# A graph network in four layers: norms, scores, logits and attention rows made group by group

## The chip, the cores and the metric

The kernel runs on one core of a Trainium2 chip. A core has TensorE (PE in the profile; its weight loads are listed apart as PEld), VectorE (DVE), ScalarE (ACT), GpSimd (POOL) and SyncE (SP, which here only issues transfers). Each takes its instructions from a queue of its own, in order, and waits there for semaphores. The metric is the device time of one execution in microseconds, the median of several.

## The reference

The input is a table of 3125 nodes with 256 features, 100,000 edges, and a second list of 65,536 edges. Eight layers follow one another; each normalises the rows (no weights), computes something, and adds it to x:

```
x += gat2(norm(x))          two attention layers with one head, over the edges and self loops
x += moe0(norm(x))          scores = n @ Wg + bg; two of 8 experts, gelu
x += norm(x) @ W            W is a 256x256 matrix set from the edge weights
x += moe1(norm(x))          routing by a 4-head attention over the second list; two of 4 experts
x += channel(norm(x))       s = n @ Wself + b; softmax per channel over a node's edges
x += moe2(norm(x))          rh = relu(n @ w1 + b1); scores = softmax(rh @ w2 + b2); two of 6
x += gat8(norm(x))          attention with 8 heads of 32, relu
x += moe3(norm(x))          the tokens are added too; scores = n @ rw; two of 8, gelu
```

An attention sums, for each node, the rows of its sources with weights exp(leaky_relu(a_src + a_dst)), divided by the sum of the weights. The channel layer does the same for each of the 256 channels apart, with weights that depend only on the source. An expert layer takes for every node the two experts with the highest scores and adds their two outputs, in most layers with a gate.

## The kernel before, in words

Nodes are padded to 3200: 25 tiles of 128 rows, in five groups of five (`GT`, `NG`), or for the multi-head attentions in seven chunks of up to four (`CHUNKS`). x stays on chip as 25 tiles of 128x256. The normalised table is kept transposed in `xT`.

`norm_group(g, then)` normalises one group: five `bn_stats` and five `bn_aggr` on DVE (L181, L183), the reciprocal square root over DVE, ACT and DVE (L184 to L186), the shift (L187), and then for each of the five tiles the normalised tile `xn` on ACT (L190), two transposes on PE (L166), their copy to `xT` on ACT (L167), and `then(t, xn)`. `xn` has five buffers, the transposes' banks `tr` two; `acc` has six. `layer_norm` (L195) runs the five groups one after another.

Edges are held as a dense table of counts in device memory, 3200x3200. `aggregate` (one head) and `channels` go over five groups of target tiles; for each they run over all 25 source tiles, load a strip of counts (L261, four buffers, on SP's queue), and collect into five accumulator banks by matmul (L294 in the first, L1406 in the second); then each of the five tiles is finished on DVE. In `aggregate_heads` (multi-head) a chunk of four tiles takes four passes over the sources with two heads each; of ten units seven form their weights on DVE (L366) and three on ACT and POOL (L360, L361, L363), and the matmul is L368. Strips of counts (L324) stay for the four passes in 25 + `kept` buffers; `kept` is 8 in the last attention. At the fourth source of the next chunk the chunk's sums are transposed back (L339) and finished (L1477 to L1482).

`gat_prepare` makes what an attention needs: weights with attention columns (L205 to L211), then for every tile the projected row (four PE matmuls at L221, a copy on ACT at L223, one on DVE at L224), and then the maximum, the exponentials and the scaling (L228 to L251).

`experts` sorts the nodes by expert, gathers rows with indirect transfers on POOL, runs the experts on PE, scatters results, and at its end combines: for each tile a load of two result rows (L680) and two DVE instructions that add them to x (L685). After each group it calls `after(g)`. `keep_row` (L444) writes a normalised tile to the table that is gathered from; it issues on SP.

A planner orders the instructions of PE, DVE, ACT and SP by modelled times. It takes the earliest in program order among those it believes ready, so it can pull later work into idle time of an engine; POOL keeps the order of the program. The channel aggregation stands in a branch on the edge data (`tc.If`), and nothing moves across the branch.

The seams in question, with their lines: after the second attention `layer_norm(keep_row)` (L1269) and `project` for 25 tiles (L432, L437); after the second expert layer's combine the logits of the channel layer (L1377, L1380, L1382, L1383; the exponentials are L1387 and the transposes back L1391); after the channel aggregation `layer_norm` and a two-layer router (L1452, L1455, L1458, L1459); after the third expert layer's combine `gat_prepare`; after the last attention `layer_norm(add_tokens)`, whose extra DVE addition is L1491, and `project` (L432, L435).

Of the kernel before, what the change touches and what calls it, by code (L numbers as in the profile page):

```python
# [41 lines left out]
AF = mybir.ActivationFunctionType  # L42
ALU = mybir.AluOpType
# [34 lines left out]
def gnn_moe_kernel(ctx: ExitStack, tc: tile.TileContext, a, out):  # L78
# [120 lines left out]
    def gat_prepare(pool, inT, w, att_src, att_dst, heads, hd, width, loops):  # L199
# [18 lines left out]
        for t in range(T):  # L218
            ps = acc_bank()
            for k in range(KD):  # L220
                nc.tensor.matmul(ps[:, :f + 2 * heads], inT[:, k, t * P:(t + 1) * P], waug[:, k, :],  # L221
                                 start=(k == 0), stop=(k == KD - 1))
            nc.scalar.copy(mov[:, t, :, 0:hd], ps[:, :f].rearrange("p (h d) -> p h d", h=heads))  # L223
            nc.vector.tensor_copy(elr[:, t, :], ps[:, f:f + 2 * heads])  # L224
        el, er = elr[:, :, 0:heads], elr[:, :, heads:]
# [31 lines left out]

    def load_counts(pool, s, c0, n):

        ct = new(pool, [P, GT * P], "ct", bufs=4)[:, :n * P]  # L260
        nc.sync.dma_start(ct, view(cnt_1)[s * P:(s + 1) * P, c0 * P:(c0 + n) * P])  # L261
        return ct
# [19 lines left out]
    def aggregate(pool, mov, q, r, finish, background):  # L282


        for g in range(NG):
# [10 lines left out]
            for j in range(GT):  # L296
                finish(g * GT + j, acc[j])

# [128 lines left out]
    def project(dst, w_sb, e, bias=None):  # L427

        for t in range(T):
            ps = tr_bank()  # L430
            for k in range(KD):
                nc.tensor.matmul(ps[:, :e], xT[:, k, t * P:(t + 1) * P], w_sb[:, k, :],  # L432
                                 start=(k == 0), stop=(k == KD - 1))
            if bias is None:
                nc.vector.tensor_copy(dst[:, t, :], ps[:, :e])  # L435
            else:
                nc.vector.tensor_add(dst[:, t, :], ps[:, :e], bias)  # L437
# [740 lines left out]
    quick.close()  # L1178
    with tc.tile_pool(name="gat1", bufs=1) as gp:
# [6 lines left out]
        aggregate(gp, mov, q, r, finish, background)  # L1186
# [80 lines left out]
    rows, keep_row = token_rows(0)  # L1267
    rows1, keep_row1 = token_rows(1)
    layer_norm(keep_row)  # L1269
    with tc.tile_pool(name="moe0", bufs=1) as mp:  # L1270
        e = 8
        wg = new(mp, [P, KD, e], "wg")
        nc.sync.dma_start(wg, a["L0_ffn_Wg"].rearrange("(k p) e -> p k e", p=P))
        bg = bcast(a["L0_ffn_bg"], e, mp, "bg")
        score = new(mp, [P, T, e], "score")
        project(score, wg, e, bg)
        oh1, _, oh2, _ = top_two(mp, score, e)

        def after0(g):
            norm_group(g)  # L1280
            for t in range(g * GT, (g + 1) * GT):
# [8 lines left out]
                a["L0_ffn_W2"], a["L0_ffn_b2"], AF.Gelu, after0, meanwhile)  # L1290
    some_left = nc.values_load(flag[0:1, 2:3], min_val=0, max_val=1)
# [5 lines left out]
    with tc.tile_pool(name="route1", bufs=1) as rp:  # L1297
# [4 lines left out]
        with tc.tile_pool(name="gat_r", bufs=1) as gp:  # L1302
# [46 lines left out]
            for kept, v in zip(hot + gate, (oh1, oh2, m1, m2)):  # L1349
                nc.vector.tensor_copy(kept, v)  # L1350
        with tc.tile_pool(name="moe1", bufs=1) as mp:
            experts(mp, rows1, list(zip(hot, gate)), e, [(a["L1_ffn_W1"], a["L1_ffn_b1"], 512)],
                    a["L1_ffn_W2"], a["L1_ffn_b2"], AF.Gelu, norm_group)


    with tc.tile_pool(name="chan", bufs=1) as cp:
# [7 lines left out]
        with tc.tile_pool(name="self", bufs=1) as sp:  # L1364
            ws = new(sp, [P, KD, D], "ws")
            nc.sync.dma_start(ws, a["L2_gnn_W_self"].rearrange("(c p) k -> p c k", p=P))
            wsT = new(sp, [P, KD, D], "wsT")
            for c in range(KD):
                transpose_to(wsT, c, ws[:, c, :])
            bs = columns(sp, a["L2_gnn_b_self"].rearrange("(c p) -> c p", p=P), KD, "bs")  # L1370
            eT = new(sp, [P, KD, NP], "eT")
            top = new(sp, [P, KD], "top")
            for c in range(KD):
                for t0, n in CHUNKS:
                    ps = acc_bank()
                    for k in range(KD):
                        nc.tensor.matmul(ps[:, :n * P], wsT[:, k, c * P:(c + 1) * P],  # L1377
                                         xT[:, k, t0 * P:(t0 + n) * P],
                                         start=(k == 0), stop=(k == KD - 1))
                    nc.scalar.activation(eT[:, c, t0 * P:(t0 + n) * P], ps[:, :n * P], AF.Identity,  # L1380
                                         bias=bs[:, c:c + 1])
                nc.vector.tensor_reduce(top[:, c:c + 1], eT[:, c, :], AX.X, ALU.max)  # L1382
# [5 lines left out]
            for t in range(T):  # L1388
# [6 lines left out]
                split(sp, mov[0][:, t], mov[1][:, t], both)  # L1395

        def channels(pool, parts_of):

            for g in range(NG):
# [9 lines left out]
                for j in range(GT):  # L1409
# [12 lines left out]
                    nc.vector.tensor_add(x[:, t, :], x[:, t, :], o)  # L1422

# [14 lines left out]
    rows, keep_row = token_rows(2)  # L1438
    layer_norm(keep_row)
    with tc.tile_pool(name="moe2", bufs=1) as mp:  # L1440
        e = 6
        rw1 = new(mp, [P, KD, P], "rw1")
        nc.sync.dma_start(rw1, a["L2_ffn_router_w1"].rearrange("(k p) h -> p k h", p=P))
        rw2 = new(mp, [P, e], "rw2")
        nc.sync.dma_start(rw2, a["L2_ffn_router_w2"])
        rb1 = columns(mp, a["L2_ffn_router_b1"].rearrange("(c p) -> c p", p=P), 1, "rb1")
        rb2 = bcast(a["L2_ffn_router_b2"], e, mp, "rb2")
        score = new(mp, [P, T, e], "score")
        for t0, n in CHUNKS:
            ps = acc_bank()  # L1450
            for k in range(KD):
                nc.tensor.matmul(ps[:, :n * P], rw1[:, k, :], xT[:, k, t0 * P:(t0 + n) * P],  # L1452
                                 start=(k == 0), stop=(k == KD - 1))
            rh = new(mp, [P, 4 * P], "rh", bufs=2)
            nc.scalar.activation(rh[:, :n * P], ps[:, :n * P], AF.Relu, bias=rb1)  # L1455
            for j in range(n):
                pl = tr_bank()
                nc.tensor.matmul(pl[:, :e], rh[:, j * P:(j + 1) * P], rw2, start=True, stop=True)  # L1458
                nc.vector.tensor_add(score[:, t0 + j, :], pl[:, :e], rb2)  # L1459
# [5 lines left out]
                a["L2_ffn_expert_w3"], a["L2_ffn_expert_b3"], AF.Relu, norm_group)  # L1465


    with tc.tile_pool(name="gat3", bufs=1) as gp:
        h, hd = 8, 32
        _, q, r, _, flat = gat_prepare(gp, xT, a["L3_gnn_W"].rearrange("f h d -> f (h d)"),  # L1470
                                   a["L3_gnn_att_src"], a["L3_gnn_att_dst"], h, hd, 64, False)
        bias = bcast(a["L3_gnn_bias"], D, gp, "bias")

        def finish(t, sums):
# [7 lines left out]
            nc.vector.scalar_tensor_tensor(x[:, t, :], o, 0.0, x[:, t, :], op0=ALU.max, op1=ALU.add)  # L1482

        aggregate_heads(gp, lambda s: view(cnt_1)[s * P:(s + 1) * P], flat, q, r, h, hd + 1, 64, finish, (2, 5, 8), 8)


    rows, keep_row = token_rows(3)

    def add_tokens(t, xn):
        keep_row(t, xn)  # L1490
        nc.vector.tensor_add(x[:, t, :], x[:, t, :], xn)  # L1491
# [6 lines left out]
    layer_norm(add_tokens)  # L1498
    with tc.tile_pool(name="moe3", bufs=1) as mp:
        e = 8  # L1500
        rw = new(mp, [e, D], "rw")
        nc.sync.dma_start(rw, a["L3_ffn_router_w"])
        ps = tr_bank()
        for k in range(KD):
            nc.tensor.transpose(ps[:, k * e:(k + 1) * e], rw[:, k * P:(k + 1) * P], ident[:e, :e])
# [67 lines left out]
```

## Time and profile before

| what | value |
|---|---|
| median of 3 runs | 4291.32 us (4287.93 to 4295.2) |
| the profiled execution, its own time | 4283.67 us |
| its span | 4281.9 us |
| PE, DVE, POOL, ACT busy | 81%, 59%, 45%, 34% |
| mean granted TensorE clock | 0.866 |

The span is from the first to the last instruction of the one execution that was profiled. A line of the timeline gives the start and length in us, engine, source line, operation, output<-inputs and count; in brackets the idle time of the engine before it and what ended that. A line of the waits gives who waited for whom, the us in all, how often, and the longest.

### The profile page before, as it was taken

What the parts mean: (1) busy time and instruction counts of PE and PEld (TensorE: products, weight loads), DVE (VectorE), ACT (ScalarE), POOL (GpSimd) and SP (SyncE); (2) the same over time, 40 slices, a digit from 0 to 9 for tenths busy, and PEclk for the clock granted to TensorE, in tenths of its full rate; (3) what the DMA queues carried; (4) which work ended last, traced back from release to release, by engine and by line L of the source; (5) the groups of instructions that cost most, each with busy time, mean ns of one, the idle gap of its engine ahead of it and who ended that gap; (6) DMA issues with size and microseconds to landing.
All of it is one profiled execution on the core that took longest, in us unless ns stands there. A gap on an engine that the chain in (4) does not pass through costs nothing. (4 is left out here: it accounts for less than half of the span.)

```text
span 4281.9 us, 49111 instructions
## 1 busy us (share of the span) xinstructions
PE 3461.9 (81%) x15922; PEld 2276.5 (53%) x15922; DVE 2529.1 (59%) x6325; ACT 1472.6 (34%) x2767; POOL 1929.4 (45%) x1581
## 2 busy tenths in 40 slices
PE   0348988799969976999699588959959999996883
PEld 0247777678837755333477267726733333344452
DVE  7789887655443123999411623262249999997223
ACT  0212212110011224898122500022238888884010
POOL 4226667777704420777243000004507777771352
PEclk9967787799959996999799699968979999996796
DMA  7455554456615654341364244415641211101345
GB/s 262 189 161 112 127 126 87 65 107 150 130 52 158 184 145 140 118 129 48 91 182 142 63 127 121 137 55 150 184 162 59 65 62 62 47 11 46 88 152 151
DMA packets 369627, 497.83 MB, mean 116 GB/s; under 512 B 85279, under 2 KB 253288, under 8 KB 369348
## 3 DMA queue, kind: packets, MB, share of 16 engines
q1 hardware_dynamic: 240304, 345.54, 27.0%
q0 software_dynamic: 83808, 88.11, 10.0%
q10 hardware_dynamic: 45236, 60.81, 4.1%
q8 instruction: 132, 2.16, 0.2%
q14 instruction: 147, 1.20, 0.1%
HBM read 402.61 MB, written 132.68 MB: 125 GB/s over the span
## 5 line engine op out<-in xcount | busy, mean ns | idle before, releaser
L363 POOL TENSOR_TENSOR p_pool<-most,ct 128x512 f32<-128x512 f32 (+1 forms) x630 | 730.9, 1163 | 487.1 <-ACT most L361 291.8
L366 DVE SCALAR_TENSOR_TENSOR p<-acc,r,ct 128x512 f32<-128x512 f32 (+1 forms) x1470 | 909.0, 686 | 40.4 <-PE acc L368 22.4
L368 PE MATMUL acc<-p,mov 128*64 128x512 f32 (+3 forms) x2940 | 910.6, 561 | 24.3 <-DVE p L366 24.3
L629 POOL DMA_INDIRECT xg<-rows,slot x244 | 245.5, 1006 | 889.0 <-PE tr L604 546.1
L368 PE MATMUL acc<-p_pool,mov 128*64 128x512 f32 (+3 forms) x1260 | 595.0, 558 | 4.3 <-POOL p_pool L363 3.7
L368 PEld LDWEIGHTS acc<-p,mov 128*64 128x64 f32 (+1 forms) x2940 | 289.5, 128 | 398.3 <-DVE p L366 236.4
L656 ACT ACTIVATE hT<-acc,bias 128x256 f32<-128x256 f32 x424 | 199.4, 473 | 818.8 <-PE acc L654 818.8
L360 ACT ACTIVATE most<-qb,minus_r 128x512 f32<-128x512 f32 (+1 forms) x630 | 423.3, 672 | 118.4 <-POOL p_pool L363 109.9
L669 POOL DMA_INDIRECT results<-ys,home x244 | 238.1, 976 | 458.3 <-DMA results<-ys,home 218.6
L361 ACT ACTIVATE most<-most,r 128x512 f32<-128x512 f32 (+1 forms) x630 | 424.6, 676 | 16.8
L811 POOL DMA_INDIRECT cnt_2a<-val,idx x192 | 319.8, 1666 | 238.8 <-DVE last L776 108.6
L811 POOL DMA_INDIRECT cnt_2b<-val,idx x192 | 324.6, 1691 | 128.7 <-DMA cnt_2b<-val,idx 71.3
L654 PE MATMUL acc<-gT_in,w 128*128 128x256 f32 x1456 | 362.1, 398 | 25.2 <-DVE gT_in L648 25.2
L664 PE MATMUL acc<-wl,hT 128*128 128x256 f32 x1456 | 381.6, 395 | 0.0
L659 DVE CAST own_hot<-mine 64x128 fp32r<-64x128 f32 x122 | 27.0, 222 | 513.0 <-PE acc L662 512.8
L654 PEld LDWEIGHTS acc<-gT_in,w 128*128 128x128 f32 x1456 | 282.5, 199 | 76.1 <-DVE gT_in L648 36.3
L1174 PE MATMUL acc<-mov,p 128*128 128x257 f32 x1250 | 304.7, 406 | 2.9 <-DVE p L279 2.9
L664 PEld LDWEIGHTS acc<-wl,hT 128*128 128x128 f32 x1456 | 257.7, 190 | 53.8 <-issue 0.7
L294 PE MATMUL acc<-mov,p 128*128 128x257 f32 x1250 | 273.1, 381 | 6.1 <-DVE p L279 6.1
L1174 PEld LDWEIGHTS acc<-mov,p 128*128 128x128 f32 x1250 | 250.4, 204 | 50.5 <-DVE p L279 10.2
L1406 PE MATMUL acc<-mov_high,ct 128*128 128x512 f32 x625 | 250.9, 401 | 30.6 <-DVE o L1418 15.3
L294 PEld LDWEIGHTS acc<-mov,p 128*128 128x128 f32 x1250 | 237.9, 191 | 40.9 <-DVE p L279 6.8
(394 smaller groups left out, 4763.9 us busy)
## 6 DMA issues: line engine op xcount, KB each, us to landing
ct<-cnt SPq DMA_DIRECT2D x250, 320.0 KB
rows<-cnt ACTq DMA_DIRECT2D x12, 3200.0 KB
cnt<-rows ACTq DMA_DIRECT2D x12, 3200.0 KB
ct<-cnt SPq DMA_DIRECT2D x150, 256.0 KB
w<-in_L_ffn_W SPq DMA_DIRECT2D x60, 512.0 KB
wl<-in_L_ffn_W SPq DMA_DIRECT2D x60, 512.0 KB
yg<-results SPq DMA_DIRECT2D x100, 256.0 KB
rows<-ktab SPq DMA_DIRECT2D x48, 512.0 KB
```

What stands on the lines that cost most here:

```text
L294: nc.tensor.matmul(acc[j][:, :D + 1], p[:, j * P:(j + 1) * P], mov[:, s, 0, :], start=(s == 0), stop=(s == T - 1))
L360: nc.scalar.activation(most, copy[:, h, :n * P], AF.Relu, bias=minus_r[:, s, head:head + 1])
L361: nc.scalar.activation(most, most, AF.Identity, bias=r[:, s, head:head + 1])
L363: nc.gpsimd.tensor_mul(p, most, ct)
L366: nc.vector.scalar_tensor_tensor(p, banks[h][:, :n * P], r[:, s, head:head + 1], ct, op0=ALU.max, op1=ALU.mult)
L368: nc.tensor.matmul(acc[h * width:(h + 1) * width, :n * P], mov[:, s, head * wide:head * wide + width], p, start=(s == 0), stop=(s == T - 1))
L629: nc.gpsimd.indirect_dma_start(out=gathered[i][:, h, :], out_offset=None, in_=rows[:, :], in_offset=bass.IndirectOffsetOnAxis(ap=slot[:, i ...
L654: nc.tensor.matmul(ph[:, :ROWS], ws[n][:, k, c * P:(c + 1) * P], src[:, k, :], start=(k == 0), stop=(k == k_in - 1))
L664: nc.tensor.matmul(py[:, h * D:(h + 1) * D], src[:, k, h * P:(h + 1) * P], ws[-1][:, k, :], start=False, stop=(k == k_in - 1))
L811: nc.gpsimd.indirect_dma_start(out=table[:, :], out_offset=bass.IndirectOffsetOnAxis(ap=idx[:, t:t + 1], axis=0), in_=val[:, t:t + 1], in_ ...
L1174: nc.tensor.matmul(acc[j][:, :D + 1], p[:, j * P:(j + 1) * P], mov[:, s, 0, :], start=(s == 0), stop=(s == T - 1))
L1406: nc.tensor.matmul(acc[j], part[:, j * P:(j + 1) * P], mov[k][:, s, :], start=(s == 0 and i == 0 and k == 0), stop=(s == T - 1 and i == le ...
```

## The change

`gat_prepare` is cut into `gat_begin`, which loads weights and returns a function that makes one tile's row, and `gat_end`. `project` does one tile. `aggregate` takes a function that it calls after each group. With these, five pieces of work are called from the stage ahead, group by group: norm and scores of the first expert layer from the second attention; the logits of the channel layer from the second expert layer's combine; norm and router of the third expert layer from inside the branch of the channel aggregation; the last attention's rows from the third expert layer's combine; norm, token addition and scores of the last expert layer from the `finish` of the last attention. The pools that hold what they make are opened earlier, and `kept` in the last attention goes from 8 to 7. The logits' maximum is taken per group and channel half, and then over the groups.

```diff
-        for t in range(T):
+
+        def tile_of_rows(t):
             ps = acc_bank()
...
+        return tile_of_rows, (heads, hd, mov, elr, flat)
...
-    def aggregate(pool, mov, q, r, finish, background):
+    def aggregate(pool, mov, q, r, finish, after, background):
...
                 finish(g * GT + j, acc[j])
+            after(g)
...
+    def scored0(t, xn):
+        keep_row(t, xn)
+        project(score0, wg, 8, t, bg)
...
-        aggregate(gp, mov, q, r, finish, background)
+        aggregate(gp, mov, q, r, finish, lambda g: norm_group(g, scored0), background)
...
-    layer_norm(keep_row)
...
-        project(score, wg, e, bg)
-        oh1, _, oh2, _ = top_two(mp, score, e)
+        oh1, _, oh2, _ = top_two(mp, score0, e)
...
+        def logits(g):
+            norm_group(g)
+            for c in range(KD):
+                for t0, n in ((g * GT, 3), (g * GT + 3, 2)):
+                    ps = acc_bank()
+                    for k in range(KD):
+                        nc.tensor.matmul(ps[:, :n * P], wsT[:, k, c * P:(c + 1) * P], xT[:, k, t0 * P:(t0 + n) * P],
+                                         start=(k == 0), stop=(k == KD - 1))
+                    nc.scalar.activation(eT[:, c, t0 * P:(t0 + n) * P], ps[:, :n * P], AF.Identity, bias=bs[:, c:c + 1])
+                nc.vector.tensor_reduce(tops[:, c, g:g + 1], eT[:, c, g * GW:(g + 1) * GW], AX.X, ALU.max)
...
-                    a["L1_ffn_W2"], a["L1_ffn_b2"], AF.Gelu, norm_group)
+                    a["L1_ffn_W2"], a["L1_ffn_b2"], AF.Gelu, logits)
...
+    def scored2(g):
+        norm_group(g, keep_row2)
+        for t0, n in ((g * GT, 3), (g * GT + 3, 2)):
+            ps = tr_bank()
+            for k in range(KD):
+                nc.tensor.matmul(ps[:, :n * P], rw1[:, k, :], xT[:, k, t0 * P:(t0 + n) * P],
+                                 start=(k == 0), stop=(k == KD - 1))
+            rh = new(rp2, [P, 3 * P], "rh", bufs=2)
+            nc.scalar.activation(rh[:, :n * P], ps[:, :n * P], AF.Relu, bias=rb1)
+            for j in range(n):
+                pl = tr_bank()
+                nc.tensor.matmul(pl[:, :6], rh[:, j * P:(j + 1) * P], rw2, start=True, stop=True)
+                nc.vector.tensor_add(score2[:, t0 + j, :], pl[:, :6], rb2)
...
                     nc.vector.tensor_add(x[:, t, :], x[:, t, :], o)
+                scored2(g)
...
-    layer_norm(keep_row)
...
+    rows_gat3, begun3 = gat_begin(last_gat.enter_context(tc.tile_pool(name="gat3_rows", bufs=1, side="right")),
+                                  xT, a["L3_gnn_W"].rearrange("f h d -> f (h d)"),
+                                  a["L3_gnn_att_src"], a["L3_gnn_att_dst"], h3, hd3, 64)
...
-                a["L2_ffn_expert_w3"], a["L2_ffn_expert_b3"], AF.Relu, norm_group)
+                a["L2_ffn_expert_w3"], a["L2_ffn_expert_b3"], AF.Relu,
+                lambda g: norm_group(g, lambda t, xn: rows_gat3(t)))
...
+    def scored3(t, xn):
+        keep_row3(t, xn)
+        nc.vector.tensor_add(x[:, t, :], x[:, t, :], xn)
+        project(score3, rwT, 8, t)
...
-        _, q, r, _, flat = gat_prepare(gp, xT, a["L3_gnn_W"].rearrange("f h d -> f (h d)"),
-                                   a["L3_gnn_att_src"], a["L3_gnn_att_dst"], h, hd, 64, False)
+        _, q, r, _, flat = gat_end(gp, begun3, False)
...
             nc.vector.scalar_tensor_tensor(x[:, t, :], o, 0.0, x[:, t, :], op0=ALU.max, op1=ALU.add)
+            if t % GT == GT - 1:
+                norm_group(t // GT, scored3)
 
-        aggregate_heads(gp, lambda s: view(cnt_1)[s * P:(s + 1) * P], flat, q, r, h, hd + 1, 64, finish, (2, 5, 8), 8)
+        aggregate_heads(gp, lambda s: view(cnt_1)[s * P:(s + 1) * P], flat, q, r, h, hd + 1, 64, finish, (2, 5, 8), 7)
...
-    layer_norm(add_tokens)
...
-        project(score, rwT, e)
```

## The prediction

> **What bounds the kernel now.** I read the page first: no engine bounds the whole.
>
> ```profile
> PE 3461.9 (81%) x15922; PEld 2276.5 (53%) x15922; DVE 2529.1 (59%) x6325; ACT 1472.6 (34%) x2767; POOL 1929.4 (45%) x1581
> PEclk9967787799959996999799699968979999996796
> ```
>
> The stages follow each other and each has its own bound, so the second view is the table of busy time by stretch, over each stage and the seam behind it. Columns: stretch, its length, busy us of PE, PE's weight load, DVE, ACT, POOL (instructions), granted clock, DMA share, GB/s.
>
> ```profile
> 892.00:1173.00 281.00, 276.26 (x1273) 240.39 (x1274) 142.75 (x262) 11.17 (x26) 210.96 (x124) 0.99 0.69 146
> 1173.00:1211.00 38.00, 33.18 (x145) 26.93 (x144) 12.38 (x59) 14.50 (x38) 8.56 (x6) 0.57 0.24 57
> 2359.00:2391.00 32.00, 12.90 (x40) 5.79 (x40) 30.74 (x108) 17.17 (x43) 0.00 (x0) 0.50 0.64 192
> 2391.00:2426.00 35.00, 27.41 (x72) 12.93 (x71) 10.27 (x18) 14.90 (x29) 0.00 (x0) 0.84 0.00 0
> 2472.00:2790.00 318.00, 297.80 (x1250) 238.94 (x1250) 81.10 (x165) 0.00 (x0) 0.00 (x0) 0.96 0.45 128
> 2790.00:2846.00 56.00, 30.42 (x129) 20.35 (x130) 33.72 (x128) 26.25 (x64) 0.00 (x0) 0.71 0.18 62
> 3133.00:3166.00 33.00, 12.98 (x40) 5.79 (x40) 30.74 (x107) 17.45 (x44) 0.00 (x0) 0.50 0.62 186
> 3166.00:3204.00 38.00, 28.62 (x110) 21.83 (x110) 9.67 (x44) 14.38 (x38) 0.00 (x0) 0.79 0.71 246
> 3213.00:3855.00 642.00, 621.22 (x2812) 253.81 (x2813) 615.70 (x1008) 549.63 (x841) 469.80 (x381) 0.98 0.16 51
> 3888.00:3936.00 48.00, 38.40 (x152) 28.94 (x153) 24.70 (x112) 21.46 (x55) 0.00 (x0) 0.51 0.20 70
> ```
>
> Read the rows in pairs. The five seams, from the last x of the stage ahead to the last score, logit or attention row, are 38, 35, 39, 38 and 48 us. In them no engine is full and the clock is about half. The stages ahead differ in what is free: the second attention (892) and the channel aggregation (2472) are full on PE; both combines (2359, 3133) are full on DVE with PE at 40%; the last attention (3213) is full on DVE (615.70 of 642) and, by its records, nearly on PE. The third view, the timeline, shows what the seams hold:
>
> ```profile
> 1190.18 20.65 PE L432 MATMUL tr<-wg,xT 128*128 128x8 f32 x96 [0.26 <-DVE score L437]
> 2410.95 3.49 DVE L1382 TENSOR_REDUCE top<-eT 128x1 f32<-128x3200 f32 x1 [12.41 <-ACT eT L1380]
> 3177.70 25.38 PE L221 MATMUL acc<-waug,xT 128*128 128x272 f32 x100 [4.81 <-DMA ct<-cnt]
> ```
>
> A projection is four matmuls a tile, 20.65/96 = 0.215 us each at half clock.
>
> **The change part by part.** Each seam shrinks to the work of its last group, and four groups' work is paid inside the stage, on the engine that is full there. Gain = old seam - new tail - price inside.
>
> *A, norm 0 and its scores in the second attention.* Old seam: L294 ends at 1173.5, last score 1211.0: 37.6. New tail: the last x is ready at 1178.8 as now; statistics to the shift take 2.0 (the sum of L181 to L187, the square root no longer behind 15 other ACT activations), five tiles at 0.83 (L190 0.59 plus L167 0.38 on ACT, overlapping) end at 1185.5, the last projection 0.85 and L437 0.17 at about 1186.7: 13.2. Price: 16 tiles' transposes (four are already placed at 1117, five are the tail's) at 2 x 0.11 (four L166 took 0.60 with a tail of 0.27, at full clock) and 20 projections at 4 x 0.107: 3.5 + 8.6 = 12.1, all on PE, which has no gap above 0.3 us there except at two group ends. DVE idles 1.28 us before each p, so its 0.6 us a tile (statistics and L437) is covered; without that cover it is 13 us. The 20 row writes go to SP past the L261 loads, four of which stay in flight at 2.17 us each: 8.7 us of cover. **-12.3**.
>
> *C, logits in the combine of the second expert layer.* Old: last L685 ends 2390.4, negated top 2425.4: 35.0. Moved: 56 L1377 matmuls (22.9 us), 14 evictions, two reductions of 3.49, now ten of about 0.75. DVE is full, so four groups' reductions delay the last x by 4 x 2 x 0.75 = 6.0. Tail: x to last xT 8.2 as now (2398.6), the group's remaining matmuls about 3 to 7 us (a group is 22.9/5 = 4.6 at full clock, 9.1 at half), eviction 0.4, reduction, top and sign 1.1: 13 to 17. Gain 35.0 - 6.0 - 15 = **-14**. The rest (exponentials, L1391) stays.
>
> *D, norm 2 and router in the channel aggregation.* Old: last x 2806.5, last score 2845.2: 38.7. Tail: statistics to shift 3.0, last xT 4.7 later, last router matmuls 1.7, L1455 0.45, two scores 0.85, add 0.3: 11.0. Behind it now stand the last attention's weights products on DVE (memset 0.70, four times L210 and L211 at 0.84), ahead of the softmax: +4.1. Price on PE: 20 tiles' transposes 4.4, router 4 x 2.15 (a group's 640 columns through four L1452 each, at the 0.43 us of 512 columns), scores 20 x 2 x 0.107 = 4.3: 17.3. The work comes some 22 us after a group's end (the finish of five tiles is 18 us on DVE), when PE's waits for L1418 (15.3 us in all) are over, so I count nothing as hidden. 38.7 - 15.1 - 17.3 = **-6**; from +0 if every transpose waits 0.3 us more, to -23 if all falls into PE's idle time.
>
> *E, the last attention's rows in the combine of the third expert layer.* Old: last x 3165.6, last L224 3203.7: 38.1, of which 4.8 wait for a weight row that queued behind L324 loads; that load now lies 300 us earlier. Tail: x to last xT 7.7 as now, ACT's five L223 +1.8, last L221 1.0, L223 and L224 0.6: 11.1, plus 20 x 0.10 on full DVE. 38.1 - 13.1 = 25; I take **-22** for the clock. The L324 loads start at 3167 as now and need 16 us for the first 25; the first p comes at about 3190 instead of 3213.5, so they are just in time.
>
> *F, norm 3 and scores in the last attention.* Old: last x 3887.9, last score 3935.7: 47.8. Tail: statistics 3.0, xT 4.7, projection and copy 1.1: 8.8. Price on DVE, per group by the rows at 3888 to 3917: L181 1.72, L183 0.43, L184 to L187 0.5, L1491 5 x 0.35, L435 5 x 0.1 = 4.9; four groups 19.6. PE adds 13 us, beside DVE. DVE now waits at each group for the square root, xn and scores; I add 1 us a group. One ct buffer less (kept 8 to 7) takes one 1.07 us step from a lead of eight: the waits here show ct only 2.3 us in all; nothing. 47.8 - 8.8 - 23.6 = **-15.4**.
>
> Sum: -12.3 - 14 - 6 - 22 - 15.4 = **-70**. The profiled execution took 4283.67 (span 4281.9), so 4214; the median of the runs, 4291.32, is 7.65 above it and this is the number compared: **4221**.
>
> **Two rules against rows.** C and E put matmuls where the clock row says 0.50. The Trainium skill, "TensorE: Matmul & The Clock Gate", Part 1, says the array's clock is halved until PE has been busy for about 3.4 us and is halved again after such a time idle. The trace agrees on warming: L221 starts at 3177.7 and the clock is full from 3182. But in 1190 to 1210 PE was busy with 8-column matmuls and stayed at half: records of busy are not enough. By the row of 3133 (half throughout) E costs 4 x 0.40 (L221's 0.254 at clock 0.79) + 0.44 = 2.0 us a tile on PE, more than the combine's 1.3 a tile; 25 tiles from 3144 end about 3195: gain 8. By the rule it warms: gain 25. I take 22, since 272 columns a matmul is what warmed it before. Second, "ScalarE: Activation LUTs", What ACT_TABLE_LOAD costs, puts a switch of set at about 2.7 us; if each group's square root in F switched sets there and back, that is 4 x 5.3 = 21 us on ACT. The trace has one load of 1.28 us at 3885 and none for the Identity and Copy activations after it; the stage between uses Relu, Identity and Copy only. I take one load.
>
> **Rivals.**
> *Half the gain: stalls in order.* Moved instructions stand in in-order queues; each wait for another engine stops p or acc behind it. For it: PE waits 2.93 us once a chunk behind the finish. Against: PE itself waited for p only 23.5 us in the whole last attention. At 0.35 us for each of 100 tiles in A, C, D, F: 35 us back, 4256.
> *Cold clock.* The two combines stay at half as their rows show: E gives 8, C 5 (its five groups' 9.1 us each fill PE): 4221 + 14 + 9 = 4244.
> *Slower: DVE behind ACT in the last attention.* ACT's L360 waits for POOL in order, up to 6.1 us:
>
> ```profile
> ACT most L360 <- POOL p_pool L363: 79.3, 122, 6.1
> DVE p L366 <- PE acc L368: 15.4, 34, 2.1
> ```
>
> A square root, five xn and one shift behind it make seven DVE waits on ACT a group, 28 in all, and DVE has no slack. At 3.1 us, half that worst wait, 87 us: 4308. It decides from 2.5 us a wait (70/28). Against it: planned order lets DVE take other p first, and L1477 waits only 2.9 us in all.
> *Nothing moves.* The planner already pulls statistics forward (L181 at 956, 1012, 1068, 1125) and might still leave the rest late: about 4291. But text order is its priority, and D is inside a branch that it can't cross.
>
> **How the numbers follow.** Forecast 0.55 (own range 4200 to 4240), half gain 0.22, cold clock 0.10, nothing 0.03, slower 0.10. Range 4195 to 4280: it leaves out slower, nothing, and a thin lower tail (D all hidden, -17, and no waits in F, -4). A measurement tells 0.2%, 8.6 us, from no change. Faster 0.87, same 0.03, slower 0.10.
>
> **What would show it.** A: L437 ends about 15 us after the last L294, and that stage is about 12 us longer. C: DVE full in the combine, tops within 17 us of the last x. D: score about 11 us after the last x, stage 17 us longer. E: L221 done within 15 us of the last x, clock above 0.5 in the combine. F: stage 20 to 24 us longer, DVE still without gaps, seam 9 us. The prediction is wrong if the last attention grows by over 40 us, or L221 still runs after the combine.

## The result and the profile after

| | before | after |
|---|---|---|
| median | 4293.26 us (4287.93 to 4297.08) | 4329.92 us (4329.29 to 4331.6) |
| ratio, 95% interval | 1 | 1.009 (1.0074 to 1.0106) |
| span of the profiled execution | 4281.9 us | 4328.1 us |

The kernel is slower by 37 us, where 70 us less were forecast. The granted clock over the whole is the same, 0.866, and the busy times of the engines are nearly so. From the page of the changed kernel, busy time and the clock in 40 slices:

```profile
PE 3471.7 (80%) x15958; PEld 2274.2 (53%) x15958; DVE 2537.1 (59%) x6334; ACT 1474.9 (34%) x2776; POOL 1926.2 (45%) x1581
PEclk9967777888877997799799879978989999988787
```

PE has 36 matmul records more and 10 us more of busy time. So nothing here says where 46 us of span went; the stages do. Line numbers have moved: L279 is now L292, L294 L307, L432 L445, L437 L450, L435 L448, L366 L380, L368 L382, L360 L374, L363 L377, L273 and L274 L286 and L287, L221 L222, L224 L225, L1406 L1463, L1382 L1392, L1491 L1529. The table of busy time by stretch, changed kernel: each stage, then what is left of its seam. Columns: stretch, length, busy us of PE, weight load, DVE, ACT, POOL (instructions), granted clock, DMA share, GB/s.

```profile
893.00:1262.00 369.00, 320.24 (x1390) 271.71 (x1390) 148.33 (x285) 21.33 (x52) 212.86 (x128) 0.87 0.54 115
1262.00:1281.00 19.00, 8.11 (x31) 5.84 (x32) 9.05 (x38) 4.58 (x11) 0.27 (x1) 0.57 0.11 36
2428.00:2464.00 36.00, 21.69 (x87) 14.33 (x88) 33.09 (x108) 21.28 (x54) 0.00 (x0) 0.75 0.57 171
2464.00:2489.00 25.00, 14.33 (x56) 8.41 (x55) 9.84 (x30) 19.86 (x42) 0.00 (x0) 0.82 0.03 7
2524.00:2860.00 336.00, 316.34 (x1362) 250.89 (x1362) 95.06 (x237) 23.05 (x53) 0.00 (x0) 0.97 0.45 129
2860.00:2892.00 32.00, 8.87 (x30) 4.99 (x28) 20.42 (x50) 6.69 (x14) 0.00 (x0) 0.64 0.10 33
3183.00:3217.00 34.00, 20.64 (x84) 15.25 (x85) 31.11 (x116) 18.81 (x50) 0.00 (x0) 0.75 0.62 184
3217.00:3234.00 17.00, 14.48 (x69) 10.71 (x67) 4.55 (x26) 10.88 (x31) 0.00 (x0) 1.00 0.84 293
3245.00:3963.00 718.00, 684.31 (x3209) 283.33 (x3210) 663.52 (x1192) 594.45 (x965) 487.86 (x420) 0.96 0.16 50
3966.00:3980.00 14.00, 7.87 (x30) 5.79 (x31) 5.67 (x22) 6.08 (x13) 0.00 (x0) 0.57 0.15 50
```

Every seam is short now. The first row is the news: 369 us where the same 1250 matmuls took 281, at a clock of 0.87 where it was 0.99. To see the net of each part, both traces are cut at the same instructions. A stage runs from its first main matmul to the end of its last (the two expert layers: from the first matmul of the sorting to the last addition to x); the seam runs from there to the first matmul of what follows (sorting, channel aggregation, last attention).

| part | stage, before to after | seam, before to after | net |
|---|---|---|---|
| A second attention | 281.1 to 368.4 | 42.6 to 23.8 | +68.5 |
| C second expert layer | 334.1 to 339.4 | 81.9 to 59.6 | -17.0 |
| D channel aggregation | 317.6 to 336.1 | 62.1 to 41.6 | -2.0 |
| E third expert layer | 313.7 to 315.4 | 48.8 to 27.6 | -19.5 |
| F last attention | 670.7 to 718.6 | 59.5 to 23.1 | +11.5 |
| last expert layer | 332.0 to 336.3 | | +4.3 |
| all the rest | | | +0.4 |

The sum, +46.2, is the difference of the spans. The last expert layer's 4 us are no part of the change that I can name: from its sorting to the start of its combine it took 293 to 300 us in the kernels below, in no order that follows an edit.

The hole in A, from PE's timeline in the changed kernel, behind the first group's last matmul:

```profile
948.17 0.81 PE L307 MATMUL acc<-mov,p 128*128 128x257 f32 x3
956.94 0.69 PE L166 MATMUL tr<-ident,xn 128*128 128x128 f32 x2 [7.96 <-ACT xn L190]
958.19 1.02 PE L445 MATMUL tr<-wg,xT 128*128 128x8 f32 x4 [0.56 <-ACT xT L167]
959.06 0.67 PE L166 MATMUL tr<-ident,xn 128*128 128x128 f32 x2
960.21 1.02 PE L445 MATMUL tr<-wg,xT 128*128 128x8 f32 x4 [0.47 <-issue]
...
966.25 1.02 PE L445 MATMUL tr<-wg,xT 128*128 128x8 f32 x4 [0.47 <-ACT xT L167]
967.12 1.31 PE L286 MATMUL tr<-ident,q 128*128 128x128 f32 x5
970.03 1.23 PE L307 MATMUL acc<-mov,p 128*128 128x257 f32 x2 [1.60 <-DVE p L292]
```

Between two groups there is no aggregation for 21 us: 8 us until the norm's first tile, five tiles at 2.01 us, and only then L286, the five transposes that spread q for the next group and without which no weight p can be made. The seam is not hidden in the stage; it is paid once per group. The same hole follows at 1027, 1105 and 1183. The four make 84 us, where the kernel before has two gaps of 4 us. The other 10 of the 87 us lie in the groups themselves: their 250 matmuls took 54.4 to 55.9 us before and take 55.9 to 57.3 now, with 3 to 6 us at half clock in each. The row of the first hole, in the columns of the table above:

```profile
949.00:970.00 21.00, 9.03 (x35) 6.62 (x35) 8.65 (x36) 5.33 (x13) 17.41 (x12) 0.62 0.31 32
```

### The profile page after: what moved, and what is told of

It is laid out like the page before. It is cut to its first block, busy times and chain, and to the rows that moved or that the text cites. A ratio compares the mean times of both kernels' runs of the same rounds, so it can differ in the third digit from the quotient of the medians.

```text
span 4328.1 us, 49211 instructions
## 1 busy us (share of the span) xinstructions
PE 3471.7 (80%) x15958; PEld 2274.2 (53%) x15958; DVE 2537.1 (59%) x6334; ACT 1474.9 (34%) x2776; POOL 1926.2 (45%) x1581
## 5 line engine op out<-in xcount | busy, mean ns | idle before, releaser
L377 POOL TENSOR_TENSOR p_pool<-most,ct 128x512 f32<-128x512 f32 (+1 forms) x630 | 731.1, 1164 | 514.7 <-ACT most L375 268.4
L382 PE MATMUL acc<-p,mov 128*64 128x512 f32 (+3 forms) x2940 | 925.9, 565 | 32.4 <-DVE p L380 32.4
L380 DVE SCALAR_TENSOR_TENSOR p<-acc,r,ct 128x512 f32<-128x512 f32 (+1 forms) x1470 | 913.5, 687 | 45.0 <-PE acc L382 26.6
L382 PE MATMUL acc<-p_pool,mov 128*64 128x512 f32 (+3 forms) x1260 | 598.4, 561 | 4.8 <-POOL p_pool L377 4.3
L382 PEld LDWEIGHTS acc<-p,mov 128*64 128x64 f32 (+1 forms) x2940 | 288.6, 129 | 403.8 <-DVE p L380 242.6
L374 ACT ACTIVATE most<-qb,minus_r 128x512 f32<-128x512 f32 (+1 forms) x630 | 423.2, 672 | 127.5 <-POOL p_pool L377 118.6
L667 PE MATMUL acc<-gT_in,w 128*128 128x256 f32 x1456 | 364.8, 400 | 25.6 <-DVE gT_in L661 23.8
L1187 PE MATMUL acc<-mov,p 128*128 128x257 f32 x1250 | 304.6, 406 | 4.2 <-DVE p L292 4.1
L307 PE MATMUL acc<-mov,p 128*128 128x257 f32 x1250 | 284.1, 391 | 13.1 <-DVE p L292 13.1
L1463 PE MATMUL acc<-mov_high,ct 128*128 128x512 f32 x625 | 252.2, 403 | 30.2 <-DMA ct<-cnt 15.2
L307 PEld LDWEIGHTS acc<-mov,p 128*128 128x128 f32 x1250 | 245.2, 197 | 52.0 <-DVE p L292 8.1
```

The costliest lines, as they stand in the source:

```text
L307: nc.tensor.matmul(acc[j][:, :D + 1], p[:, j * P:(j + 1) * P], mov[:, s, 0, :], start=(s == 0), stop=(s == T - 1))
L374: nc.scalar.activation(most, copy[:, h, :n * P], AF.Relu, bias=minus_r[:, s, head:head + 1])
L377: nc.gpsimd.tensor_mul(p, most, ct)
L380: nc.vector.scalar_tensor_tensor(p, banks[h][:, :n * P], r[:, s, head:head + 1], ct, op0=ALU.max, op1=ALU.mult)
L382: nc.tensor.matmul(acc[h * width:(h + 1) * width, :n * P], mov[:, s, head * wide:head * wide + width], p, start=(s == 0), stop=(s == T - 1))
L667: nc.tensor.matmul(ph[:, :ROWS], ws[n][:, k, c * P:(c + 1) * P], src[:, k, :], start=(k == 0), stop=(k == k_in - 1))
```

## The experiments

The experiments ran in four groups, and the kernel before ran beside each. Its median was 4287, 4285, 4285 and 4275 us, so ratios to it are compared, and a difference of ratios is turned into us at 4285.

### Is A the loss?

A undone, everything else of the change kept:

```
-        aggregate(gp, mov, q, r, finish, lambda g: norm_group(g, scored0), background)
+        aggregate(gp, mov, q, r, finish, lambda g: None, background)
...
+    layer_norm(scored0)
```

> Part A alone is undone: norm and scores of the first expert layer stand behind the second attention again, as before; C, D, E, F stay. Theory 1 (A is the loss): from the start of the second attention to its last score the changed kernel took 387 us (893 to 1280), the kernel before 319 (892 to 1211), so this run is 69 us below the changed kernel: 4261, 4255 to 4268. The stage has no hole of 21 us between groups. Rival (the stages behind carry a part of the loss, such as the last attention with its 47 us more, and A only shows it early): it falls by less than 45 us, to 4285 or more.

Measured: 4278.87 us, ratio 0.9981 (0.9972 to 0.9991), 47 us below the changed kernel. The stage is back at 282.8. The gain falls short of 69. Some 9 us of this are my edit's: it kept the projection behind each tile's transposes, and that seam took 51.8 us against 42.6 in the old form (all transposes, then all projections). The rest is scatter between executions, for all I can tell: the one that was profiled was 59 us below the changed kernel's. A second pair, below, gives 64.

### What holds the next group?

Two things could: the two `tr` banks, which are handed out in text order (each tile takes one for its transposes and one for its projection, ten turns before the q of the next group gets one), or PE's own queue, in which the five tiles stand first. One run moves q to another bank and leaves the text order alone; one leaves the bank and moves the call, so that q precedes the five tiles in the text.

```
     def q_rows(pool, q, heads, c0, n, wide=0):
...
-            ps = tr_bank()
+            ps = acc_bank() if heads == 1 and not wide else tr_bank()
```

> Everything of the change stays; one thing differs: the broadcast transposes of q for the next group are written into an acc bank instead of one of the two tr banks. Text order is untouched. Theory 1 (the two tr banks rotate in text order, so q of the next group waits for the norm and the scores of all five tiles, which use ten turns of them): q comes straight behind the group's last matmul, the four holes of 21 us shrink to the moved work's own PE time and some short waits, and the time falls to 4249 (the sum of the prediction for A, 12 below the old seam, against 69 above it: 81 less) to 4275. Theory 2 (the banks are innocent; PE takes the five tiles in text order and waits in its queue for each xT at some 1.85 us): the 8 us of lead falls away at most, 4 x 8 = 32 less: about 4298, and the ten waits of each group are still seen. Theory 3 (the planner keeps the text order): no change, 4330.

```
                                     start=(s == 0), stop=(s == T - 1))
+                if g and s == 8:
+                    after(g - 1)
...
-            after(g)
+        after(NG - 1)
```

> Everything of the change stays; in the second attention the norm and scores of group g-1 are called behind the ninth source of group g instead of at the end of group g-1; q keeps its tr bank. Theory 1 (q of the next group must not stand behind the five tiles in the tr banks): q of the next group is now ahead of them in the text, so the holes close as in the run with the acc bank: 4249 to 4275. Theory 2 (PE waits in its queue for each tile's xT): the waits only move to the middle of a group, ten a group of up to 1.85 us: 4290 to 4330.

Measured: bank 4288.72, ratio 1.0001 (0.9991 to 1.0012), 38 us less than the changed kernel; middle 4258.16, ratio 0.9941 (0.9923 to 0.9959), 64 us less. In PE's timeline of the run with another bank, q comes straight behind the last matmul, and the planner now spreads the five tiles over the next group's matmuls:

```profile
950.72 0.38 PE L307 MATMUL acc<-mov,p 128*128 128x257 f32 x1
950.93 0.71 PE L286 MATMUL acc<-ident,q 128*128 128x128 f32 x5
958.32 3.79 PE L307 MATMUL acc<-mov,p 128*128 128x257 f32 x8 [6.68 <-DVE p L292]
961.91 0.63 PE L166 MATMUL tr<-ident,xn 128*128 128x128 f32 x2
962.33 2.15 PE L307 MATMUL acc<-mov,p 128*128 128x257 f32 x6
964.32 0.51 PE L445 MATMUL tr<-wg,xT 128*128 128x8 f32 x4
```

So the bank's rotation is the cause of most of the hole, and not the planner's order, which changed without any edit to it once q had another bank. The turns of 2.01 us are gone too: between a tile's transposes and its projection now stand four aggregation matmuls, 1.03 us, and a tile follows the other every 1.48 us. Theory 2 falls. But 1.0001 is above the 4275 that theory 1 allowed: the stage took 325 us, against 299 with the call in the middle, and PE waits 6.68 us for p at each of the four borders. DVE's timeline there shows what is ahead of p (L292):

```profile
953.92 0.40 DVE L181 BATCH_NORM_STATS2 bn<-x 128x6 f32<-128x256 f32 x1
...
956.41 0.74 DVE L181 BATCH_NORM_STATS2 bn<-x 128x6 f32<-128x256 f32 x2
957.07 0.42 DVE L183 BATCH_NORM_AGGREGATE stats<-bn 128x2 f32<-128x6 f32 x5
957.42 0.85 DVE L292 SCALAR_TENSOR_TENSOR p<-qb,r,ct 128x640 f32<-128x640 f32 x1
```

Whether these statistics are the rest, or the missing lead, was asked by calling A behind the second source instead of the ninth (`s == 1`):

> As the run that calls A behind the ninth source of the next group, but behind its second source; q keeps its tr bank, projections behind each tile. It asks why the run with q in an acc bank still took 325 us for the stage when the call in the middle took 299. In the former the gap of PE between groups is 6.65 us, in the latter 3.15, and DVE does the five statistics and their aggregation (five of 0.40 and 0.42) ahead of the first weights p of the next group. Theory 1 (what is left is this DVE work standing ahead of p at the seam): behind the second source the first p's come first, the gap is 3.2 again and the stage 299 to 306. Theory 2 (the moved work needs the lead of half a group; close to the seam PE's queue waits for xn and xT with no p in reserve): the gap is 3.2 but the stage 312 to 325, the time lost inside the group.

Measured: 4258.27, ratio 0.9961 (0.9947 to 0.9975); stage 302.8 us. Theory 1 holds: against the run with the other bank the stage is 22 us shorter. PE waits 3.14 us at three borders and not at all at the first, where the other run waits 6.68 us at each of four: that is 17 of the 22, since the first weights of the next group now go ahead of 3 us of statistics that nobody waits for. The other 5 lie inside the groups. Over the stage the clock is 0.98 with the call behind the second source and 0.95 with the other bank, which points to the half clock, but no run takes them apart.

The stretch of the second attention with the call in the middle:

```profile
894.00:1193.00 299.00, 289.55 (x1385) 253.51 (x1385) 145.66 (x281) 23.07 (x53) 213.33 (x129) 0.99 0.66 142
```

The clock is 0.99 again, so the 0.87 of the changed kernel came with the holes. The stage is still 18 us longer than before: by the records PE's idle time in it rose from 4.2 to 9.5 us and its busy time from 276.9 to 289.9, which is 13 for the moved work.

### How long is the chain in the hole?

```
+        def normed0(g):
+            norm_group(g, keep_row)
+            for t in range(g * GT, (g + 1) * GT):
+                project(score0, wg, 8, t, bg)
...
+        aggregate(gp, mov, q, r, finish, normed0, background)
```

> The changed kernel with one thing moved: the five projections of a group stand behind all five tiles' transposes instead of one behind each tile; q of the next group still follows in the tr banks. Theory 1 (a hole of 21 us is the lead of 8 plus five turns of transpose, copy, projection, copy at 2.0, all of which q waits for): five transposes and copies at 0.9 and five projections at 0.6 give 7.5 instead of 10.5, 3 us less at each of five places: 15 below the changed kernel, 4315. Rival (the chain is bound by ACT's xn and xT, not by the alternation): no change, within 3.

Measured: 4315.96, ratio 1.0066 (1.0049 to 1.0083), 10 us below the changed kernel; the stage is 11 us shorter and the tail 2.4, so 2.7 at each of five places, where 3 were expected. Theory 1 holds in its mechanism. With two banks and one projection behind each tile, every tile waits for the copy of its own transposes.

### F, and what the parts are worth together

F undone: norm, addition and scores stand behind the last attention, `kept` is 8.

```
-            if t % GT == GT - 1:
-                norm_group(t // GT, scored3)
...
-        aggregate_heads(gp, ... finish, (2, 5, 8), 7)
+        aggregate_heads(gp, ... finish, (2, 5, 8), 8)
...
+    layer_norm(scored3)
```

> Part F alone is undone: norm, token addition and scores of the last expert layer stand behind the last attention, and kept is 8 again; A, C, D, E stay. By the traces the last attention grew by 47 us (671 to 718) and the seam behind it shrank by 35 (48 to 13), 12 in all, less 2 in its sorting. Theory 1 (F is a net loss): 10 us below the changed kernel: 4320, 4314 to 4326. Rival (the last expert layer, 5 us longer, was lengthened by F too): 4315. Rival (F gained as predicted and the stage's growth has another cause, the rows made earlier in E): 15 us above: 4345.

Measured: 4326.09, ratio 1.0087 (1.007 to 1.0104), equal to the changed kernel within what is measured. Its stage is 674.2, its seam 66.1 with the projections again behind each tile (59.5 in the old form). F gained nothing, and not 15; against a seam in the old form it would have lost some 7 us, by an estimate from these two seams.

A and F undone in the old form (all transposes, then all projections):

> A and F are both undone in the form of the kernel before (all transposes, then all projections); C, D and E stay. By the traces of before and after, C nets -17 (seam 82 to 60, combine 5 longer), D -2 (channel stage 19 longer, seam 21 shorter), E -20 (seam 49 to 28, combine 1 longer). Theory 1 (the losses lie in A and F, the parts are independent): 39 below the kernel before, ratio 0.991. Rival (part of the gains of C and E is eaten behind, as the last expert layer's 3 to 5 us more suggest): 30 to 34 below, 0.9925.

Measured: 4253.2, ratio 0.9921 (0.9904 to 0.9937): 34 us below the kernel before, with 39 expected; its last expert layer is 5 us longer. C, D and E bring this alone. Against the run with only F undone it is 71 us less (1.0087 to 0.9921). Of these 7 are the form of the last seam (66.1 us there, 58.9 here), so A is 64, where the traces had said 69.

Then two versions meant to keep what pays. Both call A behind the ninth source, with late projections. One undoes F; the other calls F's norm one pass behind the finish:

```
+        def hook():
+            while done:
+                g = done.pop(0)
+                norm_group(g, scored3)
+                for t in range(g * GT, (g + 1) * GT):
+                    project(score3, rwT, 8, t)
...
+                if b == 1 and s == 3:
+                    hook()
```

> A called behind the ninth source of the next group with the projections behind the five transposes; C, D, E stay; F undone in the old form. Part A with the call in the middle netted -0.6 by its trace (stage 18 longer, seam 19 shorter). Theory 1 (late projections take the 2.0 us turns out of the tail, 3 to 5 us, and out of the four groups in the middle, 1 to 2 each): A nets -8; with C, D and E 47 below the kernel before, 0.989. Rival (the middle groups wait as much as before, the tail gains 3): 42 below, 0.990; if late projections gain nothing it equals the run with A and F undone.

> As the run beside it, but with F kept and moved: the norm of a finished group is called at the fourth source of the chunk's second pass, one pass behind the finish, projections behind the five transposes; kept is 7. In the trace of the changed kernel the stage grew by 47 (41 in the runs with A changed): 26 of DVE work and 15 to 21 of idle DVE. Theory 1 (the idle time comes from finish, norm and scores falling together at the start of a chunk in the two tr banks and in PE's queue): the stage grows by some 24 to 28, the seam shrinks by 36 to 40: 10 to 14 below the run with F undone. Theory 2 (any square root, xn and projection inside the stage stalls DVE, PE and POOL by as much): stage +40, equal to the run with F undone or up to 6 above. Theory 3 (one strip buffer less, kept 7, is the cause): the stage shows waits for counts at the start of a chunk, +40.

Measured: without F 4249.08, ratio 0.9914 (0.9897 to 0.993); with F moved 4245.05, ratio 0.9903 (0.9882 to 0.9924). Both beat the kernel before and the changed one; the two cannot be told from each other, nor surely from A and F undone. A at its best is worth 2 us by the trace of the former (300.3 + 21.4 against 281.1 + 42.6). In two runs below with the same A the stage took 306.8 and 306.5 us, and there it loses 4.

For F, theory 2 is nearer. In the changed kernel the stage grew by 48 us; with the norm moved away from the finish it grew by 37, with no gap of DVE above 1.2 us at any norm. In three runs above with F as in the changed kernel it grew by 41, so the collision is some 4 us (where the other 7 come from stands further below), and the 37 need another reason. Buffers are not it:

```
-        aggregate_heads(gp, ... finish, (2, 5, 8), 8)
+        aggregate_heads(gp, ... finish, (2, 5, 8), 7)
```

> The run with A and F undone, with kept 7 in the last attention in place of 8, nothing else. Theory 1 (a strip buffer less costs nothing, as predicted): the stage takes 671 to 674 as before. Rival (it brings waits for counts): the stage is 5 to 40 longer, with waits of POOL or DVE for a count transfer in the list.

Measured, against A and F undone: 4250.98, ratio 0.9926 (0.9909 to 0.9942), and the stage took 672.1, with 1.7 us of waits for counts in all. A strip buffer less costs nothing.

Two runs take the 37 us apart, one by taking PE work out, one by adding DVE work:

```
                 norm_group(g, scored3)
-                for t in range(g * GT, (g + 1) * GT):
-                    project(score3, rwT, 8, t)
...
+    for t in range(T):
+        project(score3, rwT, 8, t)
```

> The run with F in the second pass, but its 25 projections and score copies stand behind the whole last attention; norm and token addition stay inside. In the run it is compared with, each of the four chunks with a norm is 8.3 to 9.9 us longer, PE is busy 8 us more in each and its only gap stays 2.9; the projections are 20 PE matmuls a group, 3.6 us by their records, and five copies on DVE, 0.8 us. Theory 1 (PE is the bound of this stage, and F's price is what it issues on PE): the stage falls by 4 x 3.6 to 4.5, from +37 to +19 to +23 against the kernel before. Theory 2 (DVE is the bound): it falls by 4 x 0.8, to +33. Behind the stage 20 more projections cost 5 to 15, so the whole is near the run compared with.

```
+        twice = new(rp3, [P, 2, 6], "twice")
+        for i in range(2):
+            nc.vector.bn_stats(twice[:, i, :], xn)
         nc.vector.tensor_add(x[:, t, :], x[:, t, :], xn)
```

> The run with F in the second pass, with work added: behind each normalised tile two more statistics instructions on DVE whose result nobody uses, 0.41 us each, 4.1 a group. Nothing is added on PE. Theory 1 (PE is the bound of the stage; DVE has 5 to 6 us of 112 to spare a chunk): the stage is longer by 0 to 6. Theory 2 (DVE is the bound): longer by 4 x 4.1 = 16. Theory 3 (bursts on DVE and on PE come one after the other, so that each delays the stage in full): also 16, and the stage without projections then falls by 18 to 22, not by 3.

Measured: 4249.13, ratio 0.9916 (0.99 to 0.9933), and 4260.11, ratio 0.994 (0.9923 to 0.9956). The last attention by stretch, in the order A and F undone, F in the second pass, projections out, statistics added:

```profile
3177.00:3851.00 674.00, 651.89 (x3091) 277.87 (x3091) 641.25 (x1102) 576.27 (x921) 487.53 (x420) 0.98 0.16 49
```

```profile
3176.00:3883.00 707.00, 681.13 (x3211) 291.50 (x3210) 664.91 (x1192) 593.45 (x965) 487.99 (x420) 0.98 0.16 51
```

```profile
3178.00:3871.00 693.00, 667.36 (x3130) 283.12 (x3131) 660.95 (x1173) 593.46 (x965) 487.82 (x420) 0.98 0.17 52
```

```profile
3185.40:3908.00 722.60, 692.62 (x3211) 295.11 (x3211) 676.86 (x1234) 593.69 (x966) 488.28 (x420) 0.96 0.16 50
```

The third row has 81 matmuls and 4 us of DVE less than the second, and is 14 us shorter. The fourth has not one matmul more, 12 us more of DVE by the records (16 by count and size), and is 15 us longer; but its clock is lower. So look at one pass alone, the second of the fourth chunk, in which a group is normalised. The order is A and F undone, projections out, F in the second pass, statistics added, and last a stretch inside the fourth:

```profile
3518.60:3543.20 24.60, 24.60 (x111) 9.41 (x110) 23.77 (x36) 22.21 (x34) 19.14 (x16) 1.00 0.00 0
3524.90:3554.50 29.60, 28.78 (x123) 11.30 (x122) 28.77 (x54) 26.30 (x45) 19.34 (x16) 1.00 0.07 23
3526.10:3559.40 33.30, 32.48 (x142) 13.05 (x142) 29.57 (x59) 26.18 (x45) 19.16 (x16) 1.00 0.06 20
3539.50:3577.60 38.10, 36.05 (x142) 15.21 (x142) 32.79 (x69) 26.30 (x45) 19.18 (x16) 0.87 0.05 18
3553.40:3563.60 10.20, 10.20 (x31) 5.01 (x31) 6.76 (x15) 1.66 (x3) 1.97 (x2) 0.50 0.00 0
```

The first three have the full clock. Norm and addition make the pass 5.0 us longer and DVE 5.0 us busier. The projections make it 3.7 longer again, though they add 0.8 to DVE, which now has 3.7 us idle. The 8.7 us together are more than DVE's 5.8. They are also more than the 4.1 us that ten transposes and 20 projections take on PE (from the start of each to the start of what follows, in PE's timeline of this pass). So neither engine alone is the bound, and the price lies between the larger of the two and their sum, 9.9. That is theory 3 in its main point. ACT too is 4 us busier; it keeps 3 us idle, and no run takes its part out.

The run with added statistics proves less. Its four passes with a norm are 3.5 to 4.8 us longer, about the 4.1 us that DVE got in each. But each also holds 7 or 10 us at half clock, 34 us in the four, and the run it is compared with has none in them. In the kernel before, the first pass of a chunk takes 29.4 us at full clock and 30.5 with 3.4 us at half. At that rate the 34 us cost some 11 (an estimate), of 17 in all. More DVE work made the stage longer, but whether by its own time or through the clock is not separated. PE's busy time there, 11 us more with the same instructions, fits the half clock too: "PE is full" cannot be read from records that stretch.

## Why the prediction was wrong

The range (4195 to 4280) did not hold the result, and the rival with the loss in it put it in the wrong stage. By the steps:

*A, -12.3 forecast, +68.5 measured.* This is 81 of the 116 us between the sum forecast (-70) and that of the table (+46). The failed step is the price: "Price: 16 tiles' transposes ... and 20 projections ... all on PE", with DVE's work "covered" by its idle time. It counts the moved work's duration and takes for granted that the next group's matmuls go on beside it. I never asked what the next group needs first. It is L273 and L274, q spread over the partitions, in the `tr` banks; and the moved work takes ten turns of those two banks ahead of it. What I had named in the front of this text, "the transposes' banks `tr` two", no term of the sum uses. The sentence "it can pull later work into idle time", true of the planner, does not hold for a bank that is given out in text order. The work itself was sized nearly right: 13 us more of busy PE in the run with the call in the middle, forecast 12.1. But that stage grew by 18, so even with the order mended A returns next to nothing. The tail was sized too low: 18.6 us from the last matmul to the last score, not 13.2, since a tile takes 2.0 us (transposes, copy, projection, in turn) and not the 0.83 of ACT's two activations.

*F, -15.4 forecast, +11.5 in the profile; in the medians 0 against a seam that was itself 7 us too long.* The failed step is "PE adds 13 us, beside DVE". In this stage it is not beside: the prediction's own row has PE busy in 621 of 642 us. With the 19.6 and 4 of DVE counted there, 36.6 come out; the run with F in its second pass grew by 37. Of the other 11 us of the changed kernel some 4 are the rival's mechanism at a smaller size, the norm at the chunk's start together with the finish. Its waits, changed kernel, last attention; columns: us in all, times, the longest:

```profile
POOL p_pool L377 <- PE acc L382: 177.7, 179, 14.0
ACT most L374 <- POOL p_pool L377: 88.2, 132, 5.3
DVE score L448 <- PE tr L445: 14.7, 16, 2.5
```

The slower rival had DVE waiting for ACT at 3.1 us, 28 times. What came is DVE waiting 14.7 us for PE's projections and POOL up to 14 us (7.3 before) for PE. The other 7 us are a half clock in the last of the four groups, of which this is a part:

```profile
3812.00:3826.00 14.00, 14.00 (x43) 5.93 (x44) 4.89 (x11) 4.59 (x9) 3.80 (x3) 0.50 0.00 0
```

It lasts 24 us in all, 3804 to 3828. The runs with A behind the second source and with late projections have the same 24 us at that place, and stages of 718 and 720 us; those with A undone, with q in another bank and with A behind the ninth source have 7 us of it, and 711. F's text is the same in all six, and why three of them fall into the long half clock stays open.

Keeping 7 strips at no cost was right. The sign of being wrong, "if the last attention grows by over 40 us", came true.

*C, -14 forecast, -17 measured.* The combine grew by 5.3 (forecast 6.0), and the top stands 14 us behind the last x (forecast 13 to 17).

*D, -6 forecast, -2 measured.* The stage grew by 18.5, forecast 17.3 with nothing hidden. The tail is 13.5 us from the last x to the last score, not 11, and from there to the sorting it is 4.4 us longer than before, where 4.1 were forecast for the weights products.

*E, -22 forecast, -19.5 measured.* The last attention row is copied (L225) 17 us behind the last x, forecast 13. Of the two ends of this step, gain 25 if the clock warms and 8 if it stays, the run is near the first: 0.75 in the combine and 1.00 behind it. Here the Trainium skill ("TensorE: Matmul & The Clock Gate", Part 1), by which the clock is full once PE has been busy for about 3.4 us, was the better guide than the row of the stretch before, which had no such matmuls in it. On the second rule weighed, the trace has one table load in the last attention, at 3459, as taken: the square roots behind it cost no switch.

So the mechanism of C, D and E was right, in sum near the forecast (38.5 by the traces, 42 forecast), and these three are the 34 us that the run with A and F undone keeps. The half gain and the cold clock rivals named true things (stalls in order, and 0.87 in A's stage) without their cause. The remark that the clock in the seams is "about half" was a misreading of its own rows, which give 0.51 to 0.84; no term of the sum rests on it.

## What to carry to other kernels

When work is moved into a loop, find the first instructions of the next iteration and ask which buffer, bank or queue place they share with it; a pool handed out in text order makes a short step wait for all that stands before it in the text, whatever the planner could do. Call the moved work a few steps into the next iteration, once the main chain has its reserve: here that alone was worth 64 us behind the ninth step and 55 behind the second. It does not make the work free: PE was full in this stage, and A then came out between 2 us gained and 4 lost. And where two engines feed each other through few buffers and both are nearly full, price an addition nearer to the sum over both than to the larger of the two: here 8.7 us a pass, between 5.8 and 9.9.

## What the hardware did that was not expected

The granted clock fell to 0.50 in the 14 us from 3812 to 3826, in which PE's records have no idle time at all; 43 instructions of PE run there, among them the 8-column matmuls, where the run with the call in the middle of A has 58 in 12 us at 0.93 (3740 to 3752). The pass with added statistics has the same, 10.2 us at 0.50 with PE busy throughout. So busy records do not mean a full clock; what would have kept it up was not tried. In A the holes brought the stage's clock from 0.99 to 0.87. Most of the half clock lay in the holes (0.62 in the first), where the moved work took nearly twice its time: transposes and projection 1.7 us a tile, and 0.9 between the matmuls of a running group. The rest lay in the group that followed, 3 to 6 us in each.
